# Cross-attention and a 32-expert layer on one core: the overflow code behind a branch becomes a dense pass over all experts

## The chip, the cores and the metric

The kernel runs on one core of a Trainium2 chip. The metric is the device time of one execution in microseconds (us), as the median of several runs. The profile is that of one further execution; its span runs from its first to its last instruction.

## The reference, cut to what matters

A layer of cross-attention is followed by a mixture of 32 experts, of which each of the 2048 tokens (16 blocks of 128) uses 8, and a shared expert. Both add to the input.

```python
x = x + xattn(layernorm(x), ctx, ctx)            # 32 query heads, 8 key/value heads of 16
h = layernorm(x).reshape(-1, 512)                # 2048 tokens
tidx, tw = gate(h, gate_weight, e_bias)          # 8 of 32 experts for a token, from 4 of 8 groups
comb = zeros((T, E)).at[rows, tidx].set(tw)
g = einsum('td,eid->tei', h, w1)
u = einsum('td,eid->tei', h, w3)
routed = einsum('tei,edi,te->td', silu(g) * u, w2, comb)
shared = silu(h @ shared_w1.T) * (h @ shared_w3.T) @ shared_w2.T
x = x + routed + shared
```

## The kernel before, in words

The program has three parts. `attention_small` computes the attention, the second layernorm and the gate's logits, and writes the normalized tokens into a table in DRAM, `rows` (2048 rows of 512 numbers and 32 weights). It also sets `not_small`, a flag that says that the keys are too long for a softmax without its maximum.

`experts` routes. It sorts the chosen (token, expert) pairs into slots; each expert has a fixed room of slots, given by its rank in size (`CAPS`, 138 slices of 128 slots in all). Then it runs over the slices: GpSimd gathers a slice's token rows from `rows` by index (line 1498), TensorE turns them (1512), multiplies by the two up-matrices (1534) and the down-matrix (1588), ScalarE scales by the routing weight (1597), and GpSimd scatters the result with an addition into the output in DRAM (1560). Gathers and scatters by index are software transfers[...]. There are 138 gathers and 150 scatters. The weights of an expert are loaded by SyncE (1162).

The third part stands behind a branch (line 1665). The flag `more` (written at lines 1397 to 1399) says that an expert got more tokens than its room, or that `not_small` is set. Every engine loads `more` (1659) and branches. If it is set, lines 1666 to 1675 follow: with `not_small` the whole of attention is done again in a general form (`attention_general`) and `experts` a second time; then `rest` deals with the tokens that found no slot. `rest` sorts them into tiles of 128 in three streams of experts, with a tile count that is known only at run time, and `tile_work` gathers, computes and scatters them, again with software transfers.

The order on TensorE, VectorE, ScalarE and GpSimd is written out by hand in the main part (`manual_schedule`); a planner sets the waits. What the planner has to do about a branch matters here. Transfers and engines count on semaphores, and what follows the branch waits for counts that are the same on both ways. So on the way on which the branch isn't taken, each engine adds to its semaphores what the skipped code would have added. On that way GpSimd's instructions at line 1665 are: two waits for its own work, four waits for the eight semaphores of software transfers, one instruction that waits for the last of them and then adds to all eight (it is called INC_SWDGE_SEM in the trace), and a branch to the end of the kernel. SyncE there adds to the eight semaphores of its own transfers and branches.

At the end of the kernel (line 1729 in the trace) SyncE makes twelve waits, for all transfers and engines. Every engine has a drain, and the engines meet at a barrier that GpSimd leads; GpSimd clears the semaphores, and a second barrier follows.

The main part's call is `experts(pieces[1:], in_order, ...)`, the one behind the branch `experts(pieces, ...)`; this is why line 1194 takes a list of any length out of `products`.

Of the kernel before, what the change touches and what calls it, by code (L numbers as in the profile page):

```python
# [9 lines left out]
F32 = mybir.dt.float32  # L10
# [8 lines left out]
P = 128  # L19
# [24 lines left out]
def tile_xattn_moe(  # L44
# [24 lines left out]
    NTILES = (NT * P * TOPK + E * (P - 1)) // P  # L69
    LT = -(-NTILES // NW)  # L70
    NQT = LT * NW

# [690 lines left out]
    def tile_work(ctx, token, owner, load_e):  # L763

        flat = out.rearrange("b s d -> (b s) d")
        wp = ctx.enter_context(tc.tile_pool(name="wp", bufs=1))

        wup = [wp.tile([P, 2, ND, I], F32, name=f"wup{r}") for r in range(NW)]  # L770
        wdn = [wp.tile([P, NI, D], F32, name=f"wdn{r}") for r in range(NW)]


        NG_BUF = 6
        xgs = [wp.tile([P, D + E], F32, name=f"xg{r}") for r in range(NG_BUF)]
        for t in xgs:
            nc.gpsimd.memset(t, 0.0)

        ps_gu = ctx.enter_context(tc.tile_pool(name="ps_gu", bufs=2, space=PSUM))
        ps_y = ctx.enter_context(tc.tile_pool(name="ps_y", bufs=2, space=PSUM))  # L780
        tp = ctx.enter_context(tc.tile_pool(name="tp", bufs=3))
        ps_a = ctx.enter_context(tc.tile_pool(name="ps_a", bufs=1, space=PSUM))
        ps_x = ctx.enter_context(tc.tile_pool(name="ps_x", bufs=2, space=PSUM))
        xg, xT, gus, al, aTs, last = {}, {}, {}, {}, {}, []

        def load_weights(q):
            r = q % NW
            with tc.issue_after(last[0]) if last else nullcontext():
                _, (e, new_e) = nc.values_load_multi_w_load_instructions(
                    load_e[0:1, :, q],  # L790
                    engines=[mybir.EngineType.SP],
                    min_val=0,
                    max_val=E - 1,
                    skip_runtime_bounds_check_because="experts' numbers and flags",
                    bass_reorder=False,
                )
            for dst, src in ((wup[r][:, 0], w1), (wup[r][:, 1], w3), (wdn[r], w2)):
                dma = nc.sync.dma_start(
                    dst,
                    src[bass.ds(e, 1)].rearrange("o p a b -> (o p) a b"),  # L800
                    **({} if q < NW else dict(cond=new_e, bounds_check="skip_entire_dma")),
                )
            last[:] = [dma.ins]

        def gather(q):
            t = xgs[q % NG_BUF]
            nc.gpsimd.indirect_dma_start(
                out=t,
                out_offset=None,
                in_=rows[:, :],  # L810
                in_offset=bass.IndirectOffsetOnAxis(ap=token[:, q : q + 1], axis=0),
                bounds_check=NT * P - 1,
                oob_is_err=False,
            )
            xg[q] = t

        def turn(q):
            tr = ps_x.tile([P, ND, P], F32, tag="trx", name="trx")
            for k in range(ND):
                nc.tensor.transpose(tr[:, k, :], xg[q][:, ts(k, P)], ident)  # L820
            t = tp.tile([P, ND, P], F32, tag="xT", name="xT")
            nc.scalar.copy(t, tr)
            xT[q] = t

        def up(q, ds):
            if 0 in ds:
                gus[q] = ps_gu.tile([P, 2, I], F32, tag="gu", name="gu")
            for d in ds:
                nc.tensor.matmul(
                    gus[q],  # L830
                    lhsT=xT[q][:, d, :],
                    rhs=wup[q % NW][:, :, d, :],
                    start=(d == 0),
                    stop=(d == ND - 1),
                )

        def gated(q):
            gu = gus.pop(q)
            del xT[q]
            sl = tp.tile([P, I], F32, tag="sl", name="sl")  # L840
            nc.scalar.activation(sl, gu[:, 0, :], AF.Silu)
            a = tp.tile([P, I], F32, tag="a", name="a")
            nc.vector.tensor_tensor(a, sl, gu[:, 1, :], ALU.mult)
            own = tp.tile([P, E], F32, tag="own", name="own")
            wt = tp.tile([P, 1], F32, tag="wt", name="wt")
            nc.vector.scalar_tensor_tensor(
                own,
                expert,
                owner[:, q : q + 1],
                xg.pop(q)[:, D:],  # L850
                ALU.is_equal,
                ALU.mult,
                accum_out=wt,
            )
            al[q] = a, wt

        def gated_turn(q):
            at = ps_a.tile([P, NI, P], F32, tag="at", name="at")
            for i in range(NI):
                nc.tensor.transpose(at[:, i, :], al[q][0][:, ts(i, P)], ident)  # L860
            aT = tp.tile([P, NI, P], F32, tag="aT", name="aT")
            nc.vector.tensor_copy(aT, at)
            aTs[q] = aT

        def down(q):
            aT, wt = aTs.pop(q), al.pop(q)[1]
            y = ps_y.tile([P, D], F32, tag="y", name="y")
            for i in range(NI):
                nc.tensor.matmul(
                    y,  # L870
                    lhsT=aT[:, i, :],
                    rhs=wdn[q % NW][:, i, :],
                    start=(i == 0),
                    stop=(i == NI - 1),
                )
            yw = tp.tile([P, D], F32, tag="yw", name="yw")
            nc.scalar.activation(yw, y, AF.Copy, scale=wt)
            nc.gpsimd.indirect_dma_start(
                out=flat,
                out_offset=bass.IndirectOffsetOnAxis(ap=token[:, q : q + 1], axis=0),  # L880
                in_=yw,
                in_offset=None,
                compute_op=ALU.add,
                bounds_check=NT * P - 1,
                oob_is_err=False,
            )

        def run(first, end):
            last.clear()
            for n in range(first - 4, end + 1):  # L890
                if first <= n + 4 < end:
                    gather(n + 4)
                if first <= n < end:
                    up(n, range(ND - 1))
                if first <= n - 1:
                    gated_turn(n - 1)
                if first <= n + 1 < end:
                    turn(n + 1)
                if first <= n < end:
                    up(n, [ND - 1])  # L900
                    gated(n)
                if first <= n - 1:
                    down(n - 1)
                if first <= n + 2 < end:
                    load_weights(n + 2)

        return run

    def rest():

        with ExitStack() as ctx:
            keep = ctx.enter_context(tc.tile_pool(name="keep", bufs=1))
            token = keep.tile([P, NQT], I32, name="token")
            owner = keep.tile([P, NQT], F32, name="owner")
            load_e = keep.tile([P, 2, NQT], I32, name="load_e")
            rounds = keep.tile([1, 1], I32, name="rounds")
            with ExitStack() as ph:
                rt = ph.enter_context(tc.tile_pool(name="rt", bufs=1))
                oh = ph.enter_context(tc.tile_pool(name="oh", bufs=2))
                ps_rt = ph.enter_context(tc.tile_pool(name="ps_rt", bufs=1, space=PSUM))  # L920
                ps_sm = ph.enter_context(tc.tile_pool(name="ps_sm", bufs=1, space=PSUM))

                def new(shape, name, dtype=F32, home=None):
                    return rt.tile(shape, dtype, tag=home or name, name=name)

                def iota(pattern, name, dtype):
                    n = pattern[0][1] * (pattern[1][1] if len(pattern) > 1 else 1)
                    i = new([P, n], name + "_i", I32)
                    nc.gpsimd.iota(i, pattern, base=0, channel_multiplier=0)
                    f = new([P, n], name, dtype)  # L930
                    nc.gpsimd.tensor_copy(f, i)
                    return f

                def triangle(name, op):
                    t = new([P, P], name, F16)
                    nc.gpsimd.memset(t, 0.0)
                    nc.gpsimd.affine_select(
                        t, t, [[-1, P]], op, 1.0, base=0, channel_multiplier=1
                    )
                    return t  # L940
# [792 lines left out]
```

## Time and profile before

| what | us |
|---|---|
| median of three runs | 1034.4 (1032.83 to 1034.75) |
| the profiled execution's own time | 1034.52 |
| its span | 1032.7 |
| busy in the span: TensorE, GpSimd, ScalarE, VectorE | 999.4, 508.5, 325.9, 255.2 |
| up-matmuls of the expert loop, line 1534 (1664 of them) | 501.9 |
| down-matmuls of the expert loop, line 1588 (672) | 260.1 |
| scatters, line 1560 (150), on GpSimd | 235.7 |
| gathers, line 1498 (138), on GpSimd | 145.3 |

A line of a group reads: source line, engine, operation, what it writes and reads, count, then busy time and the mean of one in ns. An engine with a q is its sequencer: branches, waits and semaphore operations are there and not counted as busy. The program's start and end have the line numbers of the launching code (1717, 1729).

### The profile page before, as it was taken

How to read it: one execution, taken by the hardware profiler on the slowest of the kernel's cores; microseconds unless marked ns; L12 is line 12 of the kernel's file. 1: busy time of each engine (PE TensorE's matmuls, PEld its weight loads, DVE VectorE, ACT ScalarE, POOL GpSimd, SP SyncE). 2: the span in 40 equal slices, each digit the busy share in tenths (PEclk: the TensorE clock that was granted, in tenths of full speed). 3: DMA queues.
4: the chain of work that ended last, by engine and by line, in shares of the span. 5: the costliest groups of instructions: out<-in, count | busy, mean ns of one | idle time of the engine just before them, and what ended most of it. 6: DMA issues, size and time to landing. Idle time of an engine off the chain costs nothing.

```text
span 1032.7 us, 12455 instructions
## 1 busy us (share of the span) xinstructions
PE 999.4 (97%) x4176; PEld 575.9 (56%) x4176; DVE 255.2 (25%) x902; ACT 325.9 (32%) x517; POOL 508.5 (49%) x658
## 2 busy tenths in 40 slices
PE   8999998999999999999999999999999999999993
PEld 5344444447666556676766666666644444444462
DVE  7887668951011000111111101101110010010100
ACT  5676612402222222232323232323222322322220
POOL 4588534732445445454545454545453445454342
PEclk9999999999999999999999999999999999999997
DMA  9011105053666757775757676767674766665541
GB/s 307 3 42 52 52 22 193 22 177 87 169 141 152 156 131 164 163 163 125 184 130 179 140 166 144 163 146 164 144 194 116 172 157 150 152 151 136 118 58 26
DMA packets 59865, 137.07 MB, mean 133 GB/s; under 512 B 12168, under 2 KB 16392, under 8 KB 59792
## 3 DMA queue, kind: packets, MB, share of 16 engines
q0 software_dynamic: 32032, 69.25, 35.5%
q1 hardware_dynamic: 27680, 66.81, 19.3%
q8 instruction: 35, 0.57, 0.2%
q14 instruction: 38, 0.31, 0.1%
q10 hardware_dynamic: 80, 0.13, 0.0%
HBM read 96.71 MB, written 46.73 MB: 139 GB/s over the span
## 4 chain that ended last, share of the span: by engine, by line
PE 64%; issue 5%; DMA 4%; POOL 3%; POOLq 0%; ACT 0%
PE gu L1534 40%; PE y L1588 19%; PE trx L1512 5%; DMA out_dram<-yw,token 4%; POOL out_dram L1560 2%; POOL xg L1498 1%; ACT xnT L1514 0%; POOLq L1560 0%; POOLq L1498 0%; POOLq L1659 0%
## 5 line engine op out<-in xcount | busy, mean ns | idle before, releaser
L1534 PE MATMUL gu<-xnT,wup 128*128 128x256 f32 (+8 forms) x1664 | 501.9, 450 | 2.4 <-ACT xnT L1514 2.4
L1534 PEld LDWEIGHTS gu<-xnT,wup 128*128 128x128 f32 x1664 | 313.1, 190 | 200.0 <-issue 134.1
L1560 POOL DMA_INDIRECT out_dram<-yw,token x150 | 235.7, 1571 | 368.0 <-ACT yw L1597 265.0
L1588 PE MATMUL y<-wdn,sa 128*128 128x512 f32 (+2 forms) x672 | 260.1, 594 | 0.0
L1545 DVE TENSOR_TENSOR sa<-sl,gu 128x256 f32<-128x256 f32 (+8 forms) x104 | 52.9, 508 | 699.0 <-PE gu L1534 681.8
L1498 POOL DMA_INDIRECT xg<-rows,token x138 | 145.3, 1053 | 61.1 <-issue 33.2
L1597 ACT ACTIVATE yw<-y,wt 128x512 f32<-128x512 f32 x138 | 94.8, 687 | 179.1 <-PE y L1588 153.9
L1588 PEld LDWEIGHTS y<-wdn,sa 128*128 128x128 f32 (+2 forms) x672 | 92.4, 171 | 72.7 <-issue 71.0
L1514 ACT COPY xnT<-trx 128x512 f32<-128x512 f32 (+3 forms) x150 | 81.3, 551 | 158.6 <-PE trx L1512 149.4
L1543 ACT ACTIVATE sl<-gu 128x256 f32<-128x256 f32 (+8 forms) x104 | 47.1, 453 | 247.7 <-PE gu L1534 243.0
L1512 PEld LDWEIGHTS trx<-ident,xg 128*128 128x128 f32 x552 | 69.0, 141 | 37.1 <-issue 26.2
L1512 PE MATMUL trx<-ident,xg 128*128 128x128 f32 x552 | 82.7, 273 | 0.0
L440 ACT ACTIVATE p<-sc 128x1024 f32<-128x1024 f32 x64 | 62.1, 1021 | 29.5 <-PE sc L430 29.5
L253 PE MATMUL gu<-xnT,sup 128*128 128x512 f32 x128 | 61.2, 617 | 3.9 <-ACT ssl L261 2.2
L1085 POOL TENSOR_SCALAR hq<-slice_q,sq 128x138 f16<-128x138 f16 x32 | 31.8, 1005 | 35.2 <-DVE sq L1386 23.0
L430 PE MATMUL sc<-qT,kz 32*128 32x512 f32 x256 | 41.8, 639 | 0.0
L253 PEld LDWEIGHTS gu<-xnT,sup 128*128 128x128 f32 x128 | 23.3, 195 | 28.4 <-issue 22.5
L446 PE MATMUL oT<-p,va 128*32 128x512 f32 x256 | 34.1, 605 | 1.1 <-DVE oTs L455 1.1
L475 POOL TENSOR_TENSOR x<-x,at 128x256 f32<-128x256 f32 x32 | 23.4, 734 | 22.8 <-DVE at L468 22.7
L1519 DVE SCALAR_TENSOR_TENSOR own<-expert,owner,xg 128x32 f32<-128x32 f32 x138 | 31.6, 246 | 0.0
L1420 PE MATMUL y<-sdn,sa 128*128 128x512 f32 x64 | 29.5, 615 | 0.0
L1083 ACT ACTIVATE ht<-hr,token 128x1024 f16<-128x1024 f16 x16 | 18.4, 1148 | 25.4 <-DVE hr L1076 22.6
(178 smaller groups left out, 468.2 us busy)
## 6 DMA issues: line engine op xcount, KB each, us to landing
wup<-in_w_dram SPq DMA_DIRECT2D x64, 512.0 KB
wdn<-in_w_dram SPq DMA_DIRECT2D x32, 512.0 KB
rows<-xn SPq DMA_DIRECT2D x16, 256.0 KB
out_dram<-x SPq DMA_DIRECT2D x16, 256.0 KB
x<-in_x_dram SPq DMA_DIRECT2D x15, 256.0 KB
out_dram<-yw,token POOLq DMA_INDIRECT x150
xg<-rows,token POOLq DMA_INDIRECT x138
cTs<-in_cT_dram SPq DMA_DIRECT2D x4, 256.0 KB
```

The lines of the kernel that those rows point to most:

```text
L253: nc.tensor.matmul(acc, lhsT=sup[:, w, d, ts(i, P)], rhs=xnT[k][:, d, :], start=(d == 0), stop=(d == ND - 1),)
L430: nc.tensor.matmul(scs[j // 2][:, j % 2], lhsT=kzs[b // 4 % 2][rows, b % 4, i, :], rhs=qTs[b][rows], start=True, stop=True, tile_position= ...
L440: nc.scalar.activation(p, sc, AF.Exp, scale=1.0 / HD**0.5)
L1498: nc.gpsimd.indirect_dma_start(out=t, out_offset=None, in_=rows[:, :], in_offset=bass.IndirectOffsetOnAxis(ap=token[:, j : j + 1], axis=0) ...
L1512: nc.tensor.transpose(tr[:, d, :], t[:, ts(d, P)], ident)
L1514: nc.scalar.copy(xnT[n % NTB][:, :, col : col + b - a], tr[:, :, a:b])
L1534: nc.tensor.matmul(acc[:, 0:m], lhsT=wup[k % NW][:, w, d, ts(i, P)], rhs=xnT[n % NTB][:, d, 0:m], start=(d == 0), stop=(d == ND - 1),)
L1543: nc.scalar.activation(banks[2][:, 0:m], acc[:, 0:m], AF.Silu)
L1545: nc.vector.tensor_tensor(acts[n % NTB][:, i, 0:m], banks[2][:, 0:m], acc[:, 0:m], ALU.mult)
L1560: ins = nc.gpsimd.indirect_dma_start(out=flat, out_offset=bass.IndirectOffsetOnAxis(ap=token2[:, k - 1 : k] if a else token[0:b, j : j + 1 ...
L1588: nc.tensor.matmul(y[c0:c1, :], lhsT=acts[n % NTB][:, i, col : col + c1 - c0], rhs=wdn[pieces[n][0] % NW][:, i, :], start=(i == 0), stop=( ...
L1597: nc.scalar.activation(yws[j], y, AF.Copy, scale=wt[:, j : j + 1])
```

## The change

`tile_work` is gone, and so are the tiles and streams in `rest` with their sizes (`NTILES`, `LT`, `NQT`). Behind the branch, `rest` now reads the routing weights back from `rows`, sets to zero the weights of all tokens that already found a slot, reads the partial output and the normalized tokens back, turns the tokens, and then does all 32 experts for all 2048 tokens, adding each expert's result with its weight. With `not_small` it first does the attention again and computes the weights anew (`all_weights`) and the shared expert; `experts` is no longer called a second time. All its transfers are issued by SyncE; none is a software transfer.

In the built program, the main part (from the start to the branch) has 6529 instructions in both versions, in the same order. On the way on which the branch isn't taken, GpSimd's four waits for software transfers and its INC_SWDGE_SEM are no longer there: two waits and the branch are left. At the end, SyncE waits for lower counts of the same semaphores. Between this branch and the end of the kernel, GpSimd's program holds 91 instructions instead of 2136 (TensorE 4887 instead of 6544, VectorE 1781 instead of 2412, ScalarE 947 instead of 2096, SyncE 496 instead of 2524).

```diff
-    def tile_work(ctx, token, owner, load_e):
...
-            nc.gpsimd.indirect_dma_start(
-                out=t,
-                out_offset=None,
-                in_=rows[:, :],
-                in_offset=bass.IndirectOffsetOnAxis(ap=token[:, q : q + 1], axis=0),
...
     def rest():
 
         with ExitStack() as ctx:
             keep = ctx.enter_context(tc.tile_pool(name="keep", bufs=1))
...
+            wp = ctx.enter_context(tc.tile_pool(name="wp", bufs=2))
+            comb = keep.tile([P, NT, E], F32, name="comb")
+            nc.sync.dma_start(comb, rows.rearrange("(t p) d -> p t d", p=P)[:, :, D:])
...
+            nc.vector.tensor_tensor(comb, comb, past, ALU.mult)
...
+                for b in range(B):
+                    nc.sync.dma_start(xs[b], out[b])
+                    xn2[b] = xnp.tile([P, D], F32, tag="xn", name="xn")
+                    nc.sync.dma_start(xn2[b], rows[ts(b, P), 0:D])
+                    gate_turn(b, ps_tr)
+
+            def expert_sum(up, dn, e=None):
+
+                for k in range(NTB):
+                    a = wp.tile([P, NI, TB], F32, tag="a", name="a")
+                    for i in range(NI):
+                        gu = [ps_gu.tile([P, TB], F32, tag="gu", name="gu") for _ in range(2)]
+                        for w in range(2):
+                            for d in range(ND):
+                                nc.tensor.matmul(
+                                    gu[w],
+                                    lhsT=up[:, w, d, ts(i, P)],
+                                    rhs=xnT[k][:, d, :],
...
+                            nc.vector.scalar_tensor_tensor(
+                                xs[b], y, comb[:, b, e : e + 1], xs[b], ALU.mult, ALU.add
+                            )
...
+            with tc.If(flag > 0):
+                attention_general()
+                all_weights(comb)
+                with ExitStack() as ph:
+                    ps_gu = ph.enter_context(tc.tile_pool(name="ps_gu", bufs=4, space=PSUM))
+                    ps_y = ph.enter_context(tc.tile_pool(name="ps_y", bufs=2, space=PSUM))
+                    expert_sum(sup, sdn)
             with ExitStack() as ph:
...
+                for e in range(E):
+                    up = wp.tile([P, 2, ND, I], F32, tag="up", name="up")
+                    dn = wp.tile([P, NI, D], F32, tag="dn", name="dn")
+                    for dst, of in ((up[:, 0], w1), (up[:, 1], w3), (dn, w2)):
+                        nc.sync.dma_start(dst, of[e])
+                    expert_sum(up, dn, e)
+            for b in range(B):
+                nc.sync.dma_start(out[b], xs[b])
...
-            n_rounds = nc.values_load(
...
-            with tc.If(n_rounds > 0), ExitStack() as ctx_r:
-                run = tile_work(ctx_r, token, owner, load_e)
-                run(0, 2 * NW)
-                with tc.If(n_rounds > 2):
-                    run(2 * NW, NTILES)
...
-            *product, product0, product1 = products
+            product, product0, product1 = products
...
-            for f in product:
-                f()
+            product()
...
     with tc.If(left > 0, preferred_fallthrough_block=False):
-        flag = nc.values_load(
...
-        with tc.If(flag > 0):
-            attention_general()
-            experts(pieces, ExitStack(), [], [])
         rest()
```

## The prediction

> **What bounds the kernel now.** I read the page from the top: busy times, the chain that ended last, then the last 20 us slice by slice, because the change lies behind a branch that stands at the very end.
>
> ```profile
> span 1032.7 us, 12455 instructions
> PE 999.4 (97%) x4176; PEld 575.9 (56%) x4176; DVE 255.2 (25%) x902; ACT 325.9 (32%) x517; POOL 508.5 (49%) x658
> ...
> q8 instruction: 35, 0.57, 0.2%
> q14 instruction: 38, 0.31, 0.1%
> ...
> PE gu L1534 40%; PE y L1588 19%; PE trx L1512 5%; DMA out_dram<-yw,token 4%; POOL out_dram L1560 2%; POOL xg L1498 1%; ACT xnT L1514 0%; POOLq L1560 0%; POOLq L1498 0%; POOLq L1659 0%
> ```
>
> TensorE is busy for 97% of the span, and the lines that carry the chain (1534, 1588, 1512) are those of the sorted expert loop. None of them is in the diff. No group of the whole list of groups has a line between 763 and 1068 (the tiles and streams) or between 1666 and 1675: with these inputs the branch at line 1665 isn't taken, and what the change rewrites never runs. So I look at how the program gets past the branch. The stretches from 1016 us on, with columns length, busy time of PE, PEld, DVE, ACT and POOL, granted clock, DMA share and GB/s:
>
> ```profile
> 1016.00:1018.00 2.00, 0.52 (x2) 0.00 (x0) 0.00 (x0) 0.69 (x1) 1.70 (x2) 1.00 0.35 62
> 1018.00:1020.00 2.00, 0.00 (x0) 0.00 (x0) 0.00 (x0) 0.00 (x0) 1.28 (x1) 0.89 0.70 85
> 1020.00:1021.00 1.00, 0.00 (x0) 0.00 (x0) 0.00 (x0) 0.00 (x0) 0.00 (x0) 0.50 0.19 36
> 1021.00:1022.00 1.00, 0.00 (x0) 0.00 (x0) 0.00 (x0) 0.00 (x0) 0.00 (x0) 0.50 0.00 0
> ...
> 1026.00:1032.00 6.00, 0.00 (x0) 0.00 (x0) 0.00 (x0) 0.00 (x0) 0.00 (x0) 0.50 0.01 1
> ```
>
> The last matmul ends near 1016.5, the last scatter's instruction (line 1560) at 1019.3, and the wires are quiet from 1021 on. Yet the span ends at 1032.7: 11.7 us in which no engine computes and next to nothing moves (0.01 of the DMA engines). The views by source line of 1665 (the branch) and 1729 (the end of the kernel), narrowed to windows, show who has them. Columns: engine (q: its sequencer), operation, count, ns least/median/most, first and last start.
>
> ```profile
> L1665 POOLq EVENT_SEMAPHORE  x2: 17/17/17, 1018.0 to 1018.1; - x2
> ...
> L1665 POOLq EVENT_SEMAPHORE  x1: 43/43/43, 1021.6 to 1021.6; - x1
> L1665 POOLq INC_SWDGE_SEM  x1: 1612/1612/1612, 1021.7 to 1021.7; - x1
> L1665 POOLq COMPARE_BRANCH  x1: 41/41/41, 1023.4 to 1023.4; - x1
> ...
> L1729 SPq EVENT_SEMAPHORE  x12: 28/28/28, 1023.3 to 1024.0; - x12
> L1729 POOLq DRAIN  x1: 5982/5982/5982, 1025.9 to 1025.9; - x1
> L1729 ACTq DRAIN  x1: 67/67/67, 1021.7 to 1021.7; - x1
> L1729 DVEq DRAIN  x1: 57/57/57, 1018.0 to 1018.0; - x1
> ```
>
> This is GpSimd's way out, one step after the other: at 1018.1 it has done its own waits; then it waits until all scatters have landed (1021.6); it adds to the eight semaphores of software transfers (1.61, to 1023.3); it branches (1023.4); 2.5 us later, at 1025.9, it starts the drain, which takes 5.98 (to 1031.9). The final barrier takes the last 0.8. SyncE could only begin its twelve waits at 1023.3, when those semaphores had been raised, and was done at 1024.1, so the drain set the end.
>
> [...] from the last branch to the drain VectorE needs 3.8 us (1014.2 to 1018.0), ScalarE 4.2 (1017.5 to 1021.7), GpSimd 2.5. [...] here queue 14 brings 0.31 MB in 38 pieces, 8 KB each, and only queue 8 has 16 KB. [...] GpSimd's first drain, ahead of all transfers, takes 0.17 us, the one after the long one 0.11. That the long one comes after 288 software transfers (150 scatters, 138 gathers) or after the semaphore addition fits both[...].
>
> **The change, part by part.**
>
> Main part of the program: the instructions up to the branch are the same in kind, number and order on all five engines, with the same waits and operands; the three products in `route` are still three, since only the call with `pieces[1:]` is left. Cost 0.
>
> Dense experts and the general path behind the branch: not run, 0. Were the branch taken, the 32 experts would cost 32 x 96 = 3072 matmuls of the shape of line 253 (617 ns), 1.9 ms by this estimate; the inputs are the same and the flag is computed as before, so I give that no chance.
>
> Removed on the way past the branch: since no software transfer is left behind it, the not-taken side has nothing to add to the software semaphores. GpSimd's wait for the last scatter (1018.2 to 1021.6), the addition (1.61) and their order before the branch go. So does the second reason for SyncE to wait: it now waits for the landings themselves, 1021.6, and with its twelve waits (0.8 in the trace) is done at 1022.4.
>
> Moved: GpSimd's code behind the branch shrinks from 2136 instructions between branch and end to 91. [...] I cost the jump at 0.1 us and not 2.5. [...] The other engines' jumps stay long, but they end at 1021.7 at the latest (ScalarE), before the transfers' end is known; that cover is gone only if the drain vanishes too.
>
> The drain itself is the unknown. Its beginning can move from 1025.9 to 1018.3. What it does may be left over from the transfers (then it stays) or from the semaphore addition (then it goes). If it stays at 5.98, it ends at 1024.3 if it begins at once, at 1025.3 if it counts from the end of the last scatter's instruction (1019.3), at 1027.6 if from the last landing (1021.6). And part of the 1.61 us may be the same work done earlier, up to +1.5. I take the middle of 1024.3 and 1027.6, which is 1026.0; ends for the range 1024.3 and 1029.1.
>
> Sum: the end of the drain moves from 1031.9 to 1026.0, the barrier stays 0.8: span 1032.7 - 5.9 = 1026.8. The profiled execution took 1034.5, 1.8 beyond its span; that stays. The runs shown have a median of 1034.4, as good as the same, so the forecast is 1034.4 - 5.9 = 1028.5. From the bounds, 2.8 to 7.6 us saved, 1026.8 to 1031.6. SyncE (1022.4) and ScalarE (1021.8) are late next, both before the drain.
>
> **Rivals.**
>
> The drain goes with the semaphore addition. For it: GpSimd is idle from 1019.3, all has landed by 1021.6, and still the drain takes 5.98 from 1025.9, next after the only instruction that adds to those semaphores; the drains without such an addition take 0.11 and 0.17. Against: those two stand where no transfer had been made or the transfers had just been drained. Then the end is SyncE's 1022.4 plus 0.8, span 1023.3, 9.4 saved: 1025.0.
>
> Nothing is gained: what the drain waits for ends by itself some 10.3 us after the last landing (1021.6 to 1031.9), whenever it begins. Against: no view shows anything active in those 10 us. Time 1034.4.
>
> Slower: the drain now begins with three or four scatters still in flight, where before all had landed 4.3 us earlier; if it handles those worse than the wait and addition did, it grows. It has from 1018.3 to 1031.9, 13.6 us, before it costs anything, more than twice its present length; at 16 us it would cost 2.4: 1036.8. Nothing shows such a length.
>
> **How the numbers follow.** The runs before spread over 1.9 us, so a difference under about 0.2%, 2.1 us, can't be told from none; that bound is at 1032.3. Chances: drain stays and begins earlier 0.70, drain goes 0.17, nothing gained 0.10, slower 0.03. The predicted time is the first, 1028.5. The range takes in the second and the first's upper end with some tenths of spread: 1024.3 to 1032.0, which leaves out the other two, 0.13, and tails. Faster 0.70 + 0.17 = 0.87, same 0.10, slower 0.03.
>
> **What would show it.** In the profile after: no semaphore addition at the branch line; GpSimd's last branch at 1018.2 and its drain within 0.3 us of it[...]; SyncE's twelve waits done by 1022.4; the matmul groups and everything before 1017 unchanged within the spread. A drain of about 6 us that begins earlier confirms the main case, one under 0.5 us the first rival, one stretched to some 13 us the second. The forecast is wrong if the main part of the program moves by itself, or if another engine's jump, now in the open, ends last.

## The result and the profile after

| | before | after |
|---|---|---|
| median, us (runs) | 1033.62 (4) | 1027.01 (4) |
| lowest to highest, us | 1032.79 to 1034.75 | 1026.05 to 1027.87 |
| the profiled execution: own time, span, us | 1034.52, 1032.7 | 1026.05, 1024.3 |

The kernel is faster by 0.65%: the ratio is 0.9935, with a 95% interval of 0.9918 to 0.9952. The median fell by 6.6 us; the forecast was 5.9.

The page of the kernel after, its span, its busy times, the two queues that bring instructions, and the chain of waits:

```profile
span 1024.3 us, 12450 instructions
...
PE 996.9 (97%) x4176; PEld 574.6 (56%) x4176; DVE 255.2 (25%) x902; ACT 325.9 (32%) x517; POOL 508.4 (50%) x658
...
q8 instruction: 35, 0.57, 0.2%
q14 instruction: 37, 0.30, 0.1%
...
PE gu L1384 36%; PE y L1438 17%; DMA out_dram<-yw,token 5%; PE trx L1362 5%; POOL out_dram L1410 3%; POOL xg L1348 2%; POOLq L1348 0%; POOLq L1410 0%; ACT xnT L1364 0%; POOLq L1509 0%
```

The same lines carry the chain, 150 lines higher up (1534 is now 1384, 1588 is 1438, 1560 is 1410), and every engine does as many operations as before. Queue 14, one of the two that bring instructions, made 37 fetches, one fewer than before. Of the spans' 8.4 us of difference, not all belongs to the change. TensorE is busy for 2.5 us less. The slices from 170 to 174 us show why, first of the kernel before, then of the kernel after (PEclk is the number behind POOL's):

```profile
170.00:172.00 2.00, 2.00 (x3) 0.80 (x3) 0.43 (x1) 0.00 (x0) 0.04 (x1) 0.50 1.02 412
172.00:174.00 2.00, 2.00 (x11) 0.88 (x10) 0.17 (x1) 0.00 (x0) 0.00 (x0) 0.74 1.02 414
```

```profile
170.00:172.00 2.00, 2.00 (x8) 0.81 (x7) 0.43 (x1) 0.00 (x0) 0.04 (x1) 1.00 1.00 399
172.00:174.00 2.00, 2.00 (x13) 1.07 (x11) 1.88 (x3) 0.00 (x0) 1.39 (x2) 1.00 1.00 406
```

TensorE's clock was granted at half for some 3 us in the first execution, not in the second; a second such stretch, at 209 to 214 us, is in both (granted clock 0.66 over these 5 us, before and after). Both kernels' times come in pairs about 1.8 us apart (1032.8 and 1034.6; 1026.1 and 1027.9). The kernel after, profiled again (run after_again, below), took 1028.05 us and has the first stretch too, so this is a draw of each execution and not the change. With that stretch its last scatter starts at 1017.95, against 1017.71 in the kernel before, so the main part didn't move. This is why I compare the tails from the start of the last scatter on. It starts at 1017.7 before and at 1015.95 after. From there to the end of the span it is 15.0 us before and 8.3 after: 6.7 us gained, as much as the medians show, so all of it lies in the tail.

The views by source line of the branch (now 1515) and of the end (now 1570), for the kernel after, narrowed to GpSimd's last stretch, to SyncE from 1016 to 1021, and to ScalarE, follow. GpSimd's long drain there is what I call its last drain; two short ones of the closing barrier come after it.

```profile
L1515 POOLq COMPARE_BRANCH  x2: 41/42/43, 1016.1 to 1016.4; - x2
L1515 POOLq EVENT_SEMAPHORE  x2: 17/17/17, 1016.2 to 1016.3; - x2
...
L1570 POOLq DRAIN  x1: 6560/6560/6560, 1016.9 to 1016.9; - x1
...
L1570 SPq EVENT_SEMAPHORE  x10: 28/28/28, 1019.1 to 1020.0; - x10
L1570 SPq DRAIN  x2: 7/10/13, 1020.0 to 1020.1; - x2
...
L1570 ACTq DRAIN  x2: 8/38/67, 1019.7 to 1023.7; - x2
```

No INC_SWDGE_SEM stands at the branch any more. GpSimd branches at 1016.4 and is at its drain 0.4 us later. The drain lasts to 1023.4. SyncE has finished its waits at 1020.0 (its own drain begins), ScalarE its jump at 1019.7; GpSimd's drain still ends last.

The drain's record grew from 5.98 to 6.56 because it begins earlier: the sequencer reaches it while the last scatter's instruction is still running on the engine (1015.95 to 1017.51). That instruction has 0.64 us to go; from its end the drain lasts 5.92.

### The profile page after: what moved, and what is told of

Its sections match the earlier page's. It is cut to its first block, busy times and chain, and to the rows that moved or that the text cites. A ratio compares the mean times of both kernels' runs of the same rounds, so it can differ in the third digit from the quotient of the medians.

```text
span 1024.3 us, 12450 instructions
## 1 busy us (share of the span) xinstructions
PE 996.9 (97%) x4176; PEld 574.6 (56%) x4176; DVE 255.2 (25%) x902; ACT 325.9 (32%) x517; POOL 508.4 (50%) x658
## 4 chain that ended last, share of the span: by engine, by line
PE 58%; issue 8%; DMA 5%; POOL 5%; POOLq 0%; ACT 0%
PE gu L1384 36%; PE y L1438 17%; DMA out_dram<-yw,token 5%; PE trx L1362 5%; POOL out_dram L1410 3%; POOL xg L1348 2%; POOLq L1348 0%; POOLq L1410 0%; ACT xnT L1364 0%; POOLq L1509 0%
## 5 line engine op out<-in xcount | busy, mean ns | idle before, releaser
L437 ACT ACTIVATE p<-sc 128x1024 f32<-128x1024 f32 x64 | 62.1, 1021 | 29.3 <-PE sc L427 29.3
```

The costliest lines, as they stand in the source:

```text
L437: nc.scalar.activation(p, sc, AF.Exp, scale=1.0 / HD**0.5)
```

## The experiments

All ratios are to the kernel before on the same chip. "The tail" is measured from the start of the last scatter to the end of GpSimd's last drain: 14.2 us before, 7.5 after.

**The kernel after again**, for comparison with the next two.

> The changed kernel once more, beside the other two on the same chip. Both theories: 6.6 us below the kernel before, the final GpSimd drain beginning 0.9 us after the last scatter's start and taking 6 to 7 us.

1026.20 us, ratio 0.993 (0.9917 to 0.9943). The drain began 0.92 us after the last scatter's start and took 6.57 us. The result repeats.

**The target of the branch far away again.** Of the removed parts this brings back only the distance, with instructions that aren't executed:

```diff
             wp = ctx.enter_context(tc.tile_pool(name="wp", bufs=2))
+            pad = keep.tile([P, 1], F32, name="pad")
+            for _ in range(600):
+                nc.gpsimd.memset(pad, 0.0)
             comb = keep.tile([P, NT, E], F32, name="comb")
```

> The changed kernel with 600 tiny GpSimd memsets behind the branch, which never run: GpSimd's target is then 691 instructions away and not 91. Theory A ([...] the drain takes its 6 us from wherever it begins): from GpSimd's branch to its drain 2.5 to 4.2 us where it was 0.42, the drain still about 6, the time 2.1 to 3.8 us above the changed kernel. Rival (the drain ends a fixed 4 us after the last landing): the drain begins later and is shorter by as much, the time within 0.5 us of the changed kernel.

1028.99 us, ratio 0.9961 (0.9949 to 0.9973), 2.8 us over the kernel after. The branch (1518) and the end (1573) of this kernel, by source line:

```profile
L1518 POOLq COMPARE_BRANCH  x1: 41/41/41, 1016.6 to 1016.6; - x1
...
L1573 POOLq DRAIN  x1: 5982/5982/5982, 1020.2 to 1020.2; - x1
```

The page's line for queue 14 has the fetch that the kernel after saves:

```profile
q14 instruction: 38, 0.31, 0.1%
```

With the target 691 instructions away, GpSimd needs 3.56 us from the branch to the drain, against 0.42 with the target 91 away. And the drain takes 5.982 us, to the nanosecond what it took before. There is no semaphore addition in this kernel, so the addition did no part of the drain's work. The last landing came at 1019.77 here, 3.7 us after the last scatter's start; the drain began 0.4 us after it, and 4.3 us after it in the kernel before: the time since the landing doesn't matter either. The tail is 10.05 us, 2.6 longer than after. That is less than the 3.1 us that the jump grew by, since the short jump only led to 0.6 us of waiting for the scatter's instruction.

**Eight software transfers behind the branch again.** These are transfers that GpSimd issues; they aren't executed, but they are ones which the not-taken way must account for:

```diff
-                    nc.sync.dma_start(xs[b], out[b])
+                    (nc.gpsimd if b < 8 else nc.sync).dma_start(xs[b], out[b])
```

> The changed kernel with 8 of the loads behind the branch issued by GpSimd and not SyncE: they never run, but the not-taken way has to wait for all scatters and add to the eight software semaphores again, with the near target kept. Theory A (the gain comes from wait and addition that stood ahead of the drain): addition of 1.6 us begins 0.1 after the last landing, the drain 0.5 after that, some 4.7 later than in the changed kernel, takes about 6: the time 4.0 to 4.8 us above the changed kernel. Rival (the drain's 6 us are caused by the addition): they would have gone in the changed kernel, which its trace denies; a weaker form, that the addition does part of the drain's work: the drain 1 to 1.6 shorter, the time 2.5 to 3.5 above.

1030.49 us, ratio 0.9969 (0.9958 to 0.998), 4.3 us over the kernel after. The same two lines of code in this kernel:

```profile
L1515 POOLq EVENT_SEMAPHORE  x1: 43/43/43, 1021.5 to 1021.5; - x1
L1515 POOLq INC_SWDGE_SEM  x1: 1612/1612/1612, 1021.6 to 1021.6; - x1
L1515 POOLq COMPARE_BRANCH  x1: 41/41/41, 1023.3 to 1023.3; - x1
...
L1570 POOLq DRAIN  x1: 5982/5982/5982, 1023.7 to 1023.7; - x1
```

The wait for the last landing and the addition of 1.61 us are back, ahead of a jump that is still short (0.42). The tail is 11.9 us, 4.4 longer than after. The kernel before had this and a jump of 2.51 instead of 0.42: 4.4 + 2.1 = 6.5 of the 6.7 us. The other 0.2 is the last landing, 3.9 us after the last scatter's start in the kernel before and 3.7 in this one.

**How the drain's time depends on what went before.** This program only gathers and drains, with groups of different size. Each group has landed before its drain.

```python
for count, wait in ((1, 4), (2, 4), (4, 4), ..., (64, 4), (128, 4), (288, 4), (64, 4), (64, 40)):
    for _ in range(count):
        nc.gpsimd.indirect_dma_start(out=xgs[n % NB], ...)
        n += 1
    for r in range(min(NB, n)):
        nc.gpsimd.tensor_copy(end[:, r : r + 1], xgs[r][:, 0:1])
    for _ in range(wait):
        nc.gpsimd.memset(pause, 0.0)
    nc.gpsimd.drain()
    nc.gpsimd.memset(pause, 0.0)
```

> A program that only gathers by index and drains; attention and experts are left out, and the output holds gathered rows. It drains GpSimd after 1, 2, 4, 8, 16, 32, 64, 128, 288, 64 and 64 gathers of 128 rows, each time when all have landed and some 4 us more have passed (some 40 before the last one). Theory A (a drain works off what each software transfer since the last drain has left): its length grows with the count, from some 0.1 us to 6 or more at 288, either evenly (0.02 us each) or up to a limit; the last two are equal, since waiting does not do the work. Rival (a drain after any software transfer takes some 6 us): 6 at every count. Second rival (the work goes on by itself after the landing): short at all counts, and shorter after the 40 us.

The drain's records, after 1, 2, 4, 8, 16, 32 and 64 gathers: 1134, 1204, 1369, 1689, 2342, 3649, 6262 ns; then after 128: 2832; after 288: 7242; after 64 again: 6262, and 6262 once more with 40 us of memsets ahead of it instead of 4. The last of these by source line:

```profile
L43 POOLq DRAIN  x2: 6262/6752/7242, 791.1 to 888.9; - x2
...
L43 POOLq DRAIN  x1: 6262/6262/6262, 1024.4 to 1024.4; - x1
```

So in this run, up to 64 gathers, the drain takes longer for each software transfer since the drain before: (6262 - 2342) / 48 = 0.082 us each. Waiting doesn't shorten it. After 128 and 288 gathers it is far less than 0.082 us for each. By that rate and the record after 64, the two drains are worth 22 and 76 transfers; that is an estimate, and no record shows why the other 106 and 212 aren't in them. All transfers in this case have 128 rows of about 2 KB, so a price for each transfer and one for each row can't be told apart. From this run I first took a fixed part of 1.05 us; that was wrong, as the last two runs show.

**A drain in the main part**, 16 slices before the last and ahead of that slice's scatters, where GpSimd has slack:

```diff
             nc.scalar.activation(yws[j], y, AF.Copy, scale=wt[:, j : j + 1])
+            if j == NS - 16:
+                nc.gpsimd.drain()
             for args in waiting:
```

> The changed kernel with one GpSimd drain in its expert loop, ahead of the scatter of the 16th slice from the end. From the program that only gathers and drains, a drain takes 1.05 us and 0.082 for each transfer since the last one that is still kept, 60 of them at the end of the changed kernel. Theory A (it is this work, and a drain in the middle takes it off): the middle drain 5 to 7.5 us, hidden, since GpSimd is only half busy; the final one 1.05 + 19 x 0.082 = 2.6 from the end of the last scatter's instruction; then it ends together with SyncE's twelve waits, 3.3 us earlier than in the changed kernel: 1022.8 where that has 1026.1. Rival (the end of the program has its own 6 us): the final drain stays at 6 and the time at the changed kernel's. Second rival (the middle drain holds up GpSimd when its scatters are due): the final drain short, but the last scatter as much later, and 0 to 7 us lost before it.

1023.59 us, ratio 0.9911 (0.9897 to 0.9925). The added drain (1449) and the last one (1572):

```profile
L1449 POOLq DRAIN  x1: 9762/9762/9762, 943.8 to 943.8; - x1
...
L1572 POOLq DRAIN  x1: 3664/3664/3664, 1016.9 to 1016.9; - x1
```

Of the 9.76 us, 3.87 are a wait for a scatter, a gather and a scatter that the engine still had in front of it (to 947.65), and 5.89 are the drain's own. The last drain falls from 6.56 to 3.66: what it took for earlier transfers is paid where it costs nothing.

**The same 8 slices before the last, and at every eighth slice.** Only the condition differs: `j == NS - 8`, and `j % 8 == 2`.

> The same with the drain ahead of the scatter of the 8th slice from the end. Theory A: final drain 1.05 + 9 x 0.082 = 1.8, behind SyncE's waits, so no more is won than with the 16th: 1022.8; if the middle drain isn't hidden so near to the end, up to 3 us more.

> The same with a drain at every eighth slice, 17 in all, the last ahead of the 8th slice from the end. Theory A: each 1.05 + 17 x 0.082 = 2.4 us, 41 in all on GpSimd, inside the time that it waits for ScalarE (265 us by the waits), so hidden: 1022.8; the final drain 1.8. Rival (a drain waits for the landing of what is in flight and so holds the gathers): each longer by 2 to 4 us, and TensorE waits for tokens: over 1026.

1023.85 us, ratio 0.9902 (0.9887 to 0.9917), and 1024.49 us, ratio 0.9907 (0.9891 to 0.9922). First the kernel with one drain 8 slices early, the added drain, the last drain, and SyncE from 1018 to 1022.2:

```profile
L1449 POOLq DRAIN  x1: 7565/7565/7565, 987.3 to 987.3; - x1
...
L1572 POOLq DRAIN  x1: 3096/3096/3096, 1018.7 to 1018.7; - x1
...
L1572 SPq EVENT_SEMAPHORE  x11: 17/28/28, 1020.7 to 1022.1; - x11
L1572 SPq DRAIN  x2: 7/10/13, 1021.9 to 1022.0; - x2
```

Then the added drains of the kernel that has seventeen:

```profile
L1449 POOLq DRAIN  x17: 5489/6857/10078, 255.8 to 987.2; - x17
```

GpSimd's last drain ends at 1021.76 and SyncE's waits for the last landing at 1021.88, and ScalarE comes out of its jump, still a far one, at 1021.86: the drain no longer sets the end alone, and more early drains bring nothing more. The seventeen took 5.5 to 10.1 us each where I had expected 2.4, which is 125 us of GpSimd's sequencer, and yet the time didn't rise: GpSimd is at work for half of the span only (50% in the kernel after).

**Beside each other.** The last kernels and the kernel after were timed in separate series, so I ran both in one.

> The kernel after, unchanged, beside the next one on the same chip: 1026.1 or 1027.9 us, a ratio of 0.993 to the kernel before.

> The kernel with one drain of GpSimd 8 slices early, beside the kernel after on the same chip. If the end is now set by the last landing: 3.3 us less than the kernel after, 1022.7 or 1024.6 us, a ratio of 0.990. If the earlier difference was one between chips: as the kernel after.

The kernel after: 1027.86 us, ratio 0.9946 (0.9932 to 0.9959). With one drain 8 slices early: 1024.76 us, ratio 0.9917 (0.9903 to 0.993). The intervals don't overlap. The medians are 3.1 us apart, the lowest runs 2.6 (1026.12 and 1023.48).

**Does the drain also wait for landings?** The long middle drains asked for it. Groups of 1, 4 and 16 gathers, once landed and once in flight. `landed` makes the same copies as before. Against the program of counts:

```diff
-        for r in range(min(NB, n)):
-            nc.gpsimd.tensor_copy(end[:, r : r + 1], xgs[r][:, 0:1])
-        for _ in range(wait):
-            nc.gpsimd.memset(pause, 0.0)
+        if wait:
+            landed(count)
         nc.gpsimd.drain()
         nc.gpsimd.memset(pause, 0.0)
+        landed(count)
```

> A program that only gathers rows (128x512 f32 each) and drains; attention, routing and experts are left out. Groups of 1, 4 and 16 gathers, each once with a copy that waits for their landing ahead of the drain and once with the drain right behind the last gather (1 and 4 of the second kind twice). Theory 'count alone': the drain's work after the end of the last gather's instruction is 1.05 us + 0.082 us for each gather, landed or not: 1.13, 1.38, 2.36 us in both kinds (on top of what the drain waits for instructions still in front of it). Rival 'also the landing': with gathers in flight the drain can't end before the last has landed, some 4.5 us after its start (the median to landing of the gathers in the kernel), so 3 to 4 us after the end of its instruction, for 1 and 4 gathers alike; for 16 the larger of that and 2.36.

The timeline of GpSimd in this program, cut to the work just ahead of a drain and the long memset just behind it. Columns: start, duration, then in brackets the idle time before; ahead of the memset at line 44 this is the drain.

```profile
5.36 0.18 POOL L29 COPY end<-xg 128x1 f32<-128x1 f32 x1 [2.48 <-DMA xg<-in_x_dram,token]
5.78 0.95 POOL L44 MEMSET pause<- 128x1024 f32 x1 [0.24 <-issue]
...
14.95 1.04 POOL L33 DMA_INDIRECT xg<-in_x_dram,token  x1 [0.16 <-issue]
18.57 0.95 POOL L44 MEMSET pause<- 128x1024 f32 x1 [2.58 <-issue]
...
49.42 1.00 POOL L33 DMA_INDIRECT xg<-in_x_dram,token  x1 [0.30 <-issue]
53.28 0.95 POOL L44 MEMSET pause<- 128x1024 f32 x1 [2.86 <-issue]
...
86.24 0.18 POOL L29 COPY end<-xg 128x1 f32<-128x1 f32 x1 [1.00 <-DMA xg<-in_x_dram,token]
87.87 0.95 POOL L44 MEMSET pause<- 128x1024 f32 x1 [1.45 <-issue]
...
126.27 0.95 POOL L44 MEMSET pause<- 128x1024 f32 x1 [6.88 <-issue]
...
159.11 0.95 POOL L44 MEMSET pause<- 128x1024 f32 x1 [4.18 <-issue]
```

One gather that has landed costs 0.24 us, sixteen 1.45 (again 0.081 each, and 0.16 beside them). One in flight costs 2.58, and 2.54 when it is repeated; four cost 2.86 and then 4.18, sixteen 6.88. What differs is the landing: the last gather of these groups landed 3.5, 3.4, 3.6, 4.9 and 7.1 us after its start. One gather in flight landed at 18.43, and the drain behind it ended at 18.50. The landing rival is right: in all five groups in flight, GpSimd's drain ended only after the last of its transfers had landed. And "count alone" had its fixed part wrong. Here it is 0.16 us where I had 1.05; in the run of counts the sequencer reached each drain while a memset of 0.95 us was still running.

**Scatters and gathers.** If a scatter cost more than a gather, that would be the 3.03 us left in the kernel with the drain 16 slices early (2 gathers and 19 scatters after it).

```diff
+        for _ in range(scatters):
+            nc.gpsimd.indirect_dma_start(out=oflat[:, :], out_offset=..., in_=add, compute_op=ALU.add, ...)
-        if wait:
-            landed(count)
+        for _ in range(24):
+            nc.gpsimd.memset(pause, 0.0)
+        nc.gpsimd.memset(end[:, 0:1], 0.0)
         nc.gpsimd.drain()
```

> A program that only gathers, scatters with an addition (both 128x512 f32) and drains; attention, routing and experts are left out. Groups of 16 gathers, 16 scatters, 32 gathers, 32 scatters, 2 gathers with 19 scatters, and 9 scatters; ahead of each drain 24 long memsets (some 23 us, so that all has landed) and one of a single column, so that the drain waits for at most 0.1 us of work in front of it. Theory 'every transfer alike': some 0.1 to 0.2 us + 0.082 us each, so 1.4, 1.4, 2.7, 2.7, 1.9, 0.9 us. Rival 'a scatter costs more', by which the 3.03 us of the kernel with one drain 16 slices early are 19 scatters and 2 gathers: 0.14 us per scatter, so 1.4, 2.4, 2.7, 4.6, 3.0, 1.4 us.

The timeline again, the long memset behind the drain, after 16 gathers, 16 scatters, 32 gathers, 32 scatters:

```profile
48.31 3.98 POOL L58 MEMSET pause<- 128x1024 f32 x4 [1.47 <-issue]
...
154.15 3.98 POOL L58 MEMSET pause<- 128x1024 f32 x4 [1.45 <-issue]
...
226.74 3.98 POOL L58 MEMSET pause<- 128x1024 f32 x4 [2.75 <-issue]
...
410.82 3.98 POOL L58 MEMSET pause<- 128x1024 f32 x4 [2.75 <-issue]
```

Scatters and gathers cost the same, and 2 gathers with 19 scatters took 1.85, 9 scatters 0.87. So "every transfer alike" holds. At these rates the kernel's drain of 5.98 us is worth (5.98 - 0.16) / 0.081, about 72 transfers; I call this estimate the drain's stock. The last drains with an added one are longer than their counts: 3.03 against 1.85 (16 early), 2.45 against 0.87 (8 early), after the wait for the last scatter's instruction is taken off. They end 0.9 and 0.4 us after the last scatter has landed.

That difference follows the number of transfers made since the drain before. The traces give it for every drain that ended soon after a landing, measured from the last semaphore signal of a software transfer to the end of the drain:

| transfers since the drain before | runs | us from the last landing to the end |
|---|---|---|
| 1 | in flight, twice | 0.07, 0.08 |
| 4 | in flight, twice | 0.20, 0.20 |
| 9 | last drain of the kernels with a drain 8 slices early, three traces | 0.41, 0.41, 0.41 |
| 12 | kernel with seventeen added drains, the last of these | 0.53 |
| 15 to 19 | the same kernel, the other sixteen | 0.67 to 0.81 |
| 16 | in flight | 0.69 |
| 21 | last drain of the kernel with a drain 16 slices early | 0.90 |

This is 0.041 us for each transfer, half of 0.081, and about 0.03 beside them. My estimate from these figures is a drain that ends at the later of two times: 0.081 us for each transfer after it could begin, or 0.041 for each after the last landing. The seventeen drains, each behind 12 to 19 transfers, were long because they waited for landings: they ended 0.53 to 0.81 us after one. The single added drains ended 2.18 us (16 early) and 2.67 (8 early) after the last landing. The second of these was profiled in two executions: 2.67 in both, while its length from the end of the scatter in front was 5.78 and 5.63. So I read them as ended by the landing too, with a stock of some 52 and 64 transfers by this estimate, and the drain at the end of the kernel after as ended by its stock of 72: there the length is 5.92 in three traces, while the time from the landing goes from 3.65 to 3.97. They come after 267, 279 and 288 transfers in all, so by this estimate some 215 aren't in the drain's time in each case.

## Why the prediction was right

- **Main part 0, dense code not run.** Right: the same operations in every engine's count, and the same start of the last scatter where the clock was alike. The spread of 1.8 us between executions is in both kernels.
- **Removed: GpSimd's wait for landings and the semaphore addition ahead of the branch.** Right, and shown by bringing them back alone: 4.3 us of time, 4.4 of the tail.
- **Moved: the jump costs 0.1 us and not 2.5.** Right in kind, 0.42 measured. The drain began 0.93 us after the last scatter's start, before that scatter's instruction was done, so the 0.3 us more than forecast cost nothing. 691 instructions of distance, a third of the former 2136, were enough to bring back a jump of 3.56 us. The 0.1 was my estimate. What the traces show of fetches: 38 on queue 14 in the two kernels with the far target, 37 in the kernel after. Between GpSimd's branch and its drain, the kernel before has one of them (one packet of 0.01 MB in the DMA view from 1023.4 to 1025.9), the kernel after none (from 1016.4 to 1016.9). How much of the 2.5 us that fetch takes isn't shown. GpSimd's jump took these 2.5 us at a time when no other packet moved, and 3.6 with the padding, while the last scatters were on their way; all far jumps of ScalarE and VectorE in the kernels before and after were also made beside moving data (the software transfers held 37 to 65% of the DMA engines' time) and took 3.8 to 4.2. No run changes this alone, so it isn't shown to be the cause.
- **The drain stays.** Right, against the first rival, that it goes with the addition (1025.0 us): the kernel with the far target has no addition and the full 5.982. The allowance of up to 1.5 us, if part of the addition is the drain's work, is refuted by the same number.
- **Its end.** This is the term that was mis-sized. I had three candidates and took the middle of the outer two: 1026.0. It was the second, "counts from the end of the last scatter's instruction", 1025.3: for the kernel after that rule gives 1017.51 + 5.98 = 1023.49, and 1023.44 was measured. This makes the saving 6.6 instead of 5.9, which is what the medians show. The 1026.0 was a compromise between the candidates, and it came within 0.7 us because they lay no more than 3.3 us apart. The forecast of 1028.5 was 1.5 above the measured 1027.0; the other 0.8 is the median before, 1034.4 in the runs shown and 1033.6 in these. The runs on the drain say why the second candidate held: from the last landing at 1019.47, 72 transfers at 0.041 us would end the drain at about 1022.5 by this estimate, a microsecond before its stock does. The candidate "counts from the last landing" had something true in it: with few transfers since an early drain (21 and 9), the last drain ended 0.90 and 0.41 us after that landing.
- **Who is late next.** I expected SyncE at 1022.4 and ScalarE at 1021.8, 4.7 and 4.1 us after the last scatter's start of 1017.7. They came at 1020.0 and 1019.7, 4.1 and 3.7 after 1015.95, both ahead of the drain. With the drain shortened by an early one, SyncE's wait for the landing took its place, and ScalarE's jump ended with it.
- **The second rival** ("nothing is gained, it ends some 10.3 us after the last landing") and **the third** (the drain grows with scatters in flight) are both refuted by the drain of 6.56 us, which ended 4.0 us after the last landing; but the third had a true core. In-flight transfers do lengthen a drain, by their landing (2.58 us behind one gather in flight, 0.24 behind one that has landed), and here, by the estimate above, that was hidden behind the larger stock.
- **A reading to correct.** I counted the record of the drain, 5.98 us, as the drain's own time. In the kernel before it was, since GpSimd had stood idle since 1019.3. In other runs the record of a drain includes its wait for the instructions in front (0.64 us after, 3.87 in the middle of the loop) and for landings (one gather in flight landed at 18.43, and the drain ended at 18.50).

## What to carry to other kernels

Read the last microseconds of a kernel by the sequencers' records, also when an engine is busy for 97% of the span: of 15 us of tail in the kernel before, 11 came after the last transfer had landed. Code behind a branch that is never taken had a price here through what the not-taken way must make up for (a wait for all software transfers and an addition, 4.3 us) and through the distance of the jump (2.1 us of the gain, 2.8 when it was brought back alone). The drain of GpSimd at the end paid for software transfers made before it (5.98 us behind 288 of them); one more drain 8 slices earlier, where GpSimd had slack (busy for 50% of the span), moved part of that out of the tail (3.1 us between the medians), and it paid only until the last landing set the end (SyncE's waits for it ended at 1021.88, the drain at 1021.76).

## What the runs showed of the hardware that I had not expected

- A drain of GpSimd whose software transfers (gathers or scatters) had all landed took 0.24 us after 1, 1.45 after 16 and 2.75 after 32 made since the drain before: 0.081 us for each, and 0.16 beside them. Waiting doesn't reduce it (6262 ns records after 64, with 4 and with 40 us of memsets ahead).
- The same drain waits for the landing of GpSimd's transfers in flight: 2.5 to 2.6 us behind a single gather, against 0.24 once it had landed. With up to 21 transfers since the drain before, it ended some 0.041 us after the landing for each: 0.07 us after 1, 0.41 after 9, 0.90 after 21.
- Not every transfer is in the drain's time: the rate above, by estimate, makes it some 72 of 288 in the kernel, and 22 of 128 and 76 of 288 landed gathers. Why the others aren't, no record shows.
- GpSimd's sequencer ran ahead of its engine: with sixteen gathers in flight the drain's record began while one gather was running and three more were still to come, 4.5 us before the engine was through with them. So a drain's record can be longer than the drain.
- Half-clock stretches of TensorE (granted clock 0.50) of some 3 us come or stay away at the same place from one execution to the next. The kernel after took 1026.05 and 1026.12 us in two profiled executions without the first stretch, 1028.05 in the one with it; times come in such pairs, some 1.8 us apart.
